# A transformer layer on one core: the maxima's small transfers issued from ScalarE instead of SyncE

## The chip, the core and the metric

The kernel runs on one core of a Trainium2 chip. The engines named here are TensorE (PE in the profile; PEld is its weight load), VectorE (DVE), ScalarE (ACT), GpSimd (POOL) and SyncE (SP), which in this kernel does nothing but issue DMA transfers. The metric is the device time of one execution in microseconds (us).

## The reference

One layer: attention, then a feed-forward product with quantised weights, each behind a layer norm and with a residual. The input is x of 4 x 512 x 1024 in float32.

```python
q = (h @ Wq).reshape(b, s, 32, 32)            # h = layernorm(x)
kv = h @ Wkv                                  # one key and value head of 32 for all query heads
scores = einsum('bqhd,bkd->bhqk', q, k) * 32**-0.5
scores = where(causal, scores + slopes * (pos_k - pos_q), -inf)
x = x + einsum('bhqk,bkd->bqhd', softmax(scores), v).reshape(b, s, 1024) @ Wo
w = (unpack_6bit(qweight) - zero_point) * scale
x = x + layernorm(x) @ w.T + ffn_bias
```

The softmax is what matters here. Per batch and head, the maximum of each query's row of scores is subtracted before the exponential.

## The kernel before, in words

**Tiling.** The 32 heads are taken in 8 groups of 4, and with 4 batches that makes 32 groups of work, i = 0 to 31. Each group passes through three functions. `queries` (L675) multiplies the normed input with the group's weights (matmuls at L682 into the tile pq), splits the result in a high and a low part (qh on ScalarE, ql on VectorE, L412 and L415), writes both to DRAM (q_d) and loads them back, turned, into the group's query stack, the tile qs: 96 rows of query parts, then 28 rows of bias terms (from qr_d), then two rows for the maxima. All of these transfers go through the helper `move` at L420, and SyncE issues them.

**Maxima.** `maxima` (L727) multiplies the first 124 rows of the stack with the keys (tile s, L739). VectorE takes the maximum of each row (L752, into mx). TensorE turns mx over (tile trm, L768). ScalarE copies it into mt (L774), which is the high part; VectorE subtracts that from trm for the low part (L779, a tile also shown as mt). Two transfers of 8 KB (qs<-mt) put these 16 x 128 values as rows 124 and 125 into the query stack. The keys hold -1 in these rows, so the second score matmul subtracts the maximum by itself.

**Attention.** `attention` (L798) multiplies keys with the whole stack of 126 rows (tile st, L820, eleven banks a group, two banks in turn), ScalarE takes the exponential (tile p, L830), GpSimd cuts off what lies behind the diagonal (L839) and adds up the blocks of keys (L861), TensorE multiplies with the values (pav, L849) and sums the denominators (den, L878). The first score matmul of a group cannot begin before both mt transfers of that group have landed.

**After attention**, from about 540 us, the 16 token tiles go through the output projection (po, L1048), the second layer norm and the feed-forward product (pf, L1168).

**The order.** All operations are first recorded as `Work` items with an engine, an estimated cost, a wished time and their dependencies. `order` lays them out on the engines by these costs, forward and backward, several times, and keeps the layout with the earliest estimated end; each engine then gets its instructions in that order and runs them strictly one after the other. A change of one cost or one engine can thus move instructions everywhere. For a transfer, `done` inside `forward` takes `ISSUE` (SP 450 ns, POOL 650 ns) off the issuing engine's time, puts the bytes on one shared DMA timeline, and counts the landing `DMA_LAT` (2000 ns) after its place on it. These are figures of the planner, not measurements. `move` always issues from SyncE:

```python
def move(dst, src):
    return nc.sync.dma_start(out=dst.bitcast(F32), in_=src.bitcast(F32))
```

Of the kernel before, what the change touches and what calls it, by code (L numbers as in the profile page):

```python
# [32 lines left out]
F32 = mybir.dt.float32  # L33
# [21 lines left out]
R_MAX = R_BIAS + N_BIAS  # L55
# [63 lines left out]
class Work:  # L119
# [2 lines left out]

    LAT = {"PE": 250, "ACT": 170, "DVE": 170, "POOL": 170, "SP": 0}
    SAME = {"PE": 0, "ACT": 150, "DVE": 110, "POOL": 110, "SP": 0}
    ISSUE = {"SP": 450, "POOL": 650}
    DMA_LAT = 2000
    EARLY = 12e3
    TURN = 105
# [119 lines left out]
    def forward(self, wanted, hold=None):  # L248

        n = len(self.ops)  # L250
        seen = [0.0] * n
        mine = [0.0] * n
        shared = {"dma": 0.0, "port": 0.0}

        def first(o):
            t = max(o.hold, hold[o.n] - self.EARLY) if o.size and hold else o.hold
            for m in o.before:
                a = self.ops[m]
                t = max(t, mine[m] if a.eng == o.eng and not a.size else seen[m])
            return t  # L260

        def done(o, s):
            if o.size:
                free = s + self.ISSUE[o.eng]
                shared["dma"] = max(shared["dma"], free) + o.size / self.DMA_RATE
                seen[o.n] = shared["dma"] + self.DMA_LAT
                return free
            if o.port:
                if o.eng == "DVE":
                    s = max(s, shared["port"])  # L270
                else:
                    shared["port"] = s + o.cost
            mine[o.n] = s + o.cost + self.SAME[o.eng]
            seen[o.n] = s + o.cost + o.lat
            return s + o.cost

        edges = [[] for _ in self.ops]
        for o in self.ops:
            for m in o.before:
                edges[m].append(o.n)  # L280
        start = self.line(edges, first, wanted, done)
        self.edges = edges
        return start, max(seen)

    def backward(self, start):
# [4 lines left out]
        def takes(o):  # L290
            return self.ISSUE[o.eng] if o.size else o.cost

# [49 lines left out]
def layer_kernel(  # L342
# [14 lines left out]
    nc = tc.nc  # L357
    B = x.shape[0]
    NT = S // P
# [21 lines left out]
    def new(pool_name, tag, shape, dt, name):  # L381

        p, bufs = pools[pool_name]
        return work.item(lambda: p.tile(shape, dt, tag=tag, name=name), (pool_name + tag, bufs))
# [8 lines left out]
    def pe(at, cols, fn, out, ins, more=0.0, tiled=False):  # L393

        o = work.op("PE", at, sum(c / 2.4 + 14.0 for c in cols) + more, fn, out, ins)
        o.wt, o.tiled = len(cols), tiled

    def act(at, n, fn, out, ins, sbuf=False):
        work.op("ACT", at, n / 1.2 + (90.0 if sbuf else 70.0), fn, out, ins)

    def dve(at, n, fn, out, ins, port=False, more=0.0):
        work.op("DVE", at, n / 0.96 + 75.0 + more, fn, out, ins, port=port)
# [4 lines left out]
    def dma(at, size, fn, out, ins, eng="SP"):  # L407
        work.op(eng, at, 0.0, fn, out, ins, size=size)
# [7 lines left out]
            [lo_it], [src_it, hi_it], port=port,  # L416
        )

    def move(dst, src):
        return nc.sync.dma_start(out=dst.bitcast(F32), in_=src.bitcast(F32))  # L420


    qr_d = tc.dram_tile([NG, N_BIAS, GH, S], F32R, name="qr_d")
# [19 lines left out]
        out=mask(),  # L443
        in_=mask(),
# [230 lines left out]
    def queries(at, i):  # L675
# [18 lines left out]
        for s, src in enumerate((qh, ql)):  # L694
            dma(
                at + 0.6 + 0.7 * s, 262e3,
                lambda s=s, src=src: move(q_d[i % 4, s], src()), [q_i[i % 4][s]], [src],
            )
        for h, n, q in qs[i]:
            dma(  # L700
                at + 1.0, 57e3 * n,
                lambda h=h, n=n, q=q: move(q()[R_BIAS:R_MAX, :, :], qr_d[g, :, h : h + n, :]),
                [(q, "b")], [qr_i[g]],
            )
            for r in range(3):
                dma(
                    at + 3.0 + 0.1 * r, 65e3 * n,
                    lambda r=r, h=h, n=n, q=q: move(
                        q()[ts(r, HD), :, :],
                        q_d[i % 4, r % 2, h * HD : (h + n) * HD].rearrange(  # L710
                            "(h d) q -> d h q", d=HD
                        ),
                    ),
                    [(q, r)], [q_i[i % 4][r % 2]],
                )

    def part(i, h):

        return next((q, h - first) for first, n, q in qs[i] if first <= h < first + n)
# [7 lines left out]
    def maxima(at, i):  # L727
        b = i // NG
        k = kst[b % 2]
        mx = new("small", "mx", [P, GH * NT], F32, f"mx_{i}")  # L730
        for n, bank in enumerate(S_BANKS):
            ps = new("ps_s", "s", [P, S], F32, f"s_{i}_{n}")
            widths = [(t + 1) * P for t, _ in bank]
            places = [sum(widths[:m]) for m in range(len(bank))]

            def products(ps=ps, bank=bank, widths=widths, places=places):
                for (t, h), W, o in zip(bank, widths, places):
                    q, at = part(i, h)
                    nc.tensor.matmul(  # L739
                        ps()[:, o : o + W], q()[0:R_MAX, at, ts(t, P)], k()[0:R_MAX, :W],  # L740
                        start=True, stop=True,
                    )
            pe(
                at + 1.2 * n, widths, products, [ps],
                [(q, r) for q in {part(i, h)[0] for _, h in bank} for r in ROWS] + [k],
                more=sum(45.0 if w == P else 5.0 for w in widths),
            )
            for (t, h), W, o in zip(bank, widths, places):
                junk = new("q1", "junk", [P, S], F32, f"junk_{i}_{t}_{h}")
                dve(  # L750
                    at + 1.2 * n + 0.3, W,
                    lambda ps=ps, junk=junk, t=t, h=h, W=W, o=o: nc.vector.tensor_tensor_reduce(  # L752
                        out=junk()[:, :W],
                        in0=ps()[:, o : o + W],
                        in1=mask()[:, S - W :],
                        scale=1.0,
                        scalar=-3e38,
                        op0=ALU.add,
                        op1=ALU.max,
                        accum_out=mx()[:, h * NT + t : h * NT + t + 1],  # L760
                    ),
                    [(mx, (t, h))], [ps], more=125.0,
                )
        at += 1.2 * len(S_BANKS)
        N = GH * NT
        tr = new("ps_misc", "misc", [P, P], F32, f"trm_{i}")
        pe(
            at, [P], lambda: nc.tensor.transpose(tr()[0:N, :], mx(), ident()), [tr], [mx]  # L768
        )
        for s in range(2):  # L770
            m = new("mt", f"mt{s}", [N, P], F32R, f"mt{s}_{i}")
            if s == 0:
                hi = m
                act(at + 0.2, P, lambda: nc.scalar.copy(hi(), tr()[0:N, :]), [hi], [tr])  # L774
            else:
                lo = m
                dve(
                    at + 0.4, P,
                    lambda: nc.vector.tensor_tensor(  # L779
                        lo(), tr()[0:N, :], hi().bitcast(F32), ALU.subtract  # L780
                    ),
                    [lo], [tr, hi],
                )
            for h, n, q in qs[i]:
                dma(
                    at + 0.5 + 0.2 * s, 2e3 * n,
                    lambda m=m, s=s, h=h, n=n, q=q: move(
                        q()[R_MAX + s : R_MAX + s + 1, :, :], m()[h * NT : (h + n) * NT, :]
                    ),
                    [(q, f"m{s}")], [m],  # L790
                )


# [436 lines left out]
    for b in range(B):  # L1230
        T = T0 + b * NG * STEP
        if b:
            for t in range(NT):
                load_x(T - 3.0 * STEP + 3.0 * t, b, t)
            for t in range(NT):
                layernorm(T - 2.0 * STEP + 3.0 * t, b, t)
        for c in range(KC):
            chunk(
                T - 4.0 + 0.5 * c if b == 0 else T - 0.9 * STEP + 1.3 * c - 2.6, b, c
            )  # L1240
        keys_values(T + 6.0 if b == 0 else T - 1.0, b)
        for g in range(NG):
            i = b * NG + g
            at = T0 + i * STEP
            queries(at, i)
            maxima(at + 17.0, i)
            attention(at + 34.0, i)
        invert(T + NG * STEP + 48.0, b)
# [52 lines left out]
```

## Time and profile before

| | us |
|---|---|
| median of 3 timed runs | 828.68 (827.39 to 829.8) |
| the profiled execution, whole | 830.86 |
| its span | 828.9 |
| TensorE busy in the span | 802.1 (97%) |
| VectorE, ScalarE, GpSimd busy | 572.4, 369.4, 515.7 |
| mt transfers, count and duration of an issue | 64, median 0.514 |
| score matmuls (L820), exponentials (L830) | 352 each |

The span runs from the first to the last instruction of the program; the whole execution has a little more around it. Busy shares are of the span. A matmul's duration is counted to its modelled end, so that successive matmuls overlap: those of 512 columns take 0.39 to 0.40 us each by their rows, and follow each other every 0.23 us. A TensorE that is busy 97% of the time is therefore not working at its peak for 97% of it. SyncE's rows (SPq) are the issues of transfers; the duration of such a row is the time that the issue holds SyncE, not the transfer itself. The clock row (PEclk) tells which share of full speed TensorE was granted.

### The profile page before, as it was taken

What the parts mean: (1) busy time and instruction counts of PE and PEld (TensorE: products, weight loads), DVE (VectorE), ACT (ScalarE), POOL (GpSimd) and SP (SyncE); (2) the same over time, 40 slices, a digit from 0 to 9 for tenths busy, and PEclk for the clock granted to TensorE, in tenths of its full rate; (3) what the DMA queues carried; (4) which work ended last, traced back from release to release, by engine and by line L of the source; (5) the groups of instructions that cost most, each with busy time, mean ns of one, the idle gap of its engine ahead of it and who ended that gap; (6) DMA issues with size and microseconds to landing.
All of it is one profiled execution on the core that took longest, in us unless ns stands there. A gap on an engine that the chain in (4) does not pass through costs nothing.

```text
span 828.9 us, 13434 instructions
## 1 busy us (share of the span) xinstructions
PE 802.1 (97%) x4480; PEld 595.8 (72%) x4480; DVE 572.4 (69%) x1491; ACT 369.4 (45%) x659; POOL 515.7 (62%) x442
## 2 busy tenths in 40 slices
PE   5989999999999999999999999999999999999997
PEld 5766677776566767666766667667888888888885
DVE  7576876478676469866358656645988867678755
ACT  4336664545665354755365564340142323333320
POOL 4337968285968185876388997778556445554323
PEclk9989999999999999999999999999999999999999
DMA  7997662486742397463457774626975675565321
GB/s 221 245 249 214 186 173 63 123 221 216 207 112 82 91 257 227 116 162 113 153 138 220 200 215 141 232 51 165 254 169 137 138 184 127 137 164 131 102 51 51
DMA packets 131796, 133.39 MB, mean 161 GB/s; under 512 B 42964, under 2 KB 93140, under 8 KB 130704
## 3 DMA queue, kind: packets, MB, share of 16 engines
q1 hardware_dynamic: 130912, 129.01, 57.4%
q0 software_dynamic: 816, 3.53, 1.5%
q8 instruction: 35, 0.57, 0.3%
q14 instruction: 33, 0.27, 0.1%
HBM read 85.58 MB, written 39.85 MB: 151 GB/s over the span
## 4 chain that ended last, share of the span: by engine, by line
PE 87%; DMA 4%; DVE 4%; issue 2%; POOL 1%; ACT 1%; SPq 0%; DVEq 0%; ACTq 0%; POOLq 0%
PE po L1048 21%; PE pq L682 18%; PE pf L1168 13%; PE s L739 9%; PE st L820 9%; PE pav L849 8%; PE den L878 3%; PE pkv L616 2%; PE tr L598 2%; DVE junk L752 2%; POOL p L861 1%; DMA q_d<-ql 1%; DMA qs<-q_d 1%; ACT p L830 1%; DMA qs<-qr_d 1%
## 5 line engine op out<-in xcount | busy, mean ns | idle before, releaser
L752 DVE CUSTOM_DVE_ANT_0 junk<-s,mask 128x256 f32<-128x256 f32 (+3 forms) x512 | 250.4, 489 | 123.2 <-PE s L739 92.1
L861 POOL TENSOR_TENSOR p<-p,p 128x1536 f32<-128x1536 f32 (+2 forms) x96 | 230.4, 2400 | 20.2 <-PE pav L849 18.2
L830 ACT ACTIVATE p<-st 128x512 f32<-128x512 f32 (+1 forms) x352 | 184.0, 560 | 115.1 <-PE st L820 111.7
L682 PE MATMUL pq<-xc,wqh 128*128 128x512 f32 x512 | 195.8, 402 | 1.5 <-DVE ql L415 1.4
L1048 PE MATMUL po<-woh,aT 128*128 128x512 f32 x512 | 165.7, 390 | 0.0
L839 POOL TENSOR_SCALAR_AFFINE_SELECT p<-p 128x512 f32<-128x512 f32 x128 | 81.9, 645 | 104.4 <-ACT p L830 103.7
L739 PE MATMUL s<-kst,qs 124*128 124x256 f32 (+3 forms) x512 | 138.4, 339 | 7.0 <-DVE mx L752 3.3
L820 PE MATMUL st<-qs,kst 126*128 126x512 f32 (+1 forms) x352 | 125.6, 395 | 3.1 <-ACT p L830 2.6
L1168 PE MATMUL pf<-wf,xT 128*128 128x512 f32 x512 | 120.8, 390 | 0.7 <-DVE xT L415 0.7
L739 PEld LDWEIGHTS s<-kst,qs 124*128 124x128 f32 x512 | 89.0, 193 | 44.1 <-DVE mx L752 16.3
L682 PEld LDWEIGHTS pq<-xc,wqh 128*128 128x128 f32 x512 | 97.6, 191 | 21.6 <-DVE ql L415 2.1
L1048 PEld LDWEIGHTS po<-woh,aT 128*128 128x128 f32 x512 | 96.2, 188 | 21.4 <-ACT a L867 0.8
L1168 PEld LDWEIGHTS pf<-wf,xT 128*128 128x128 f32 x512 | 95.8, 188 | 21.5 <-DVE xT L415 1.7
L682 PE MATMUL pq<-xc,wql 128*128 128x512 f32 x256 | 101.6, 397 | 0.0
L1048 PE MATMUL po<-wol,aT 128*128 128x512 f32 x256 | 99.7, 390 | 0.0
L820 PEld LDWEIGHTS st<-qs,kst 126*128 126x128 f32 x352 | 65.0, 190 | 24.1 <-ACT p L830 9.7
L849 PE MATMUL pav<-p,kv 128*32 128x512 f32 (+3 forms) x1024 | 79.4, 436 | 0.4 <-POOL p L839 0.4
L849 PEld LDWEIGHTS pav<-p,kv 128*32 128x32 f32 x1024 | 29.9, 109 | 50.7 <-issue 38.0
L1188 POOL TENSOR_TENSOR x<-x,y 128x512 f32<-128x512 f32 x30 | 43.0, 1438 | 26.4 <-DVE y L1179 26.4
L1048 PEld LDWEIGHTS po<-wol,aT 128*128 128x128 f32 x256 | 48.1, 188 | 9.6
L1146 POOL TENSOR_TENSOR x<-x,rows 128x512 f32<-128x512 f32 x32 | 43.9, 1391 | 17.3 <-issue 10.1
L682 PEld LDWEIGHTS pq<-xc,wql 128*128 128x128 f32 x256 | 49.0, 191 | 5.8
(92 smaller groups left out, 850.5 us busy)
## 6 DMA issues: line engine op xcount, KB each, us to landing
qs<-q_d SPq DMA_DIRECT2D x96, 256.0 KB
x<-_attn_hidden_states_dram SPq DMA_DIRECT2D x31, 512.0 KB
q_d<-qh SPq DMA_DIRECT2D x32, 256.0 KB
q_d<-ql SPq DMA_DIRECT2D x32, 256.0 KB
at_d<-a SPq DMA_DIRECT2D x32, 256.0 KB
raw<-at_d SPq DMA_DIRECT2D x16, 512.0 KB
raw<-rden_d SPq DMA_DIRECT2D x64, 128.0 KB
out_dram<-x SPq DMA_DIRECT2D x32, 256.0 KB
```

The source lines that it names most:

```text
L682: nc.tensor.matmul(pq(), w()[:, c, :], xc[b, c]()[:, s, :], start=(c == 0 and n == 0), stop=(c == KC - 1 and n == 2),)
L739: nc.tensor.matmul(ps()[:, o : o + W], q()[0:R_MAX, at, ts(t, P)], k()[0:R_MAX, :W], start=True, stop=True,)
L752: lambda ps=ps, junk=junk, t=t, h=h, W=W, o=o: nc.vector.tensor_tensor_reduce(out=junk()[:, :W], in0=ps()[:, o : o + W], in1=mask()[:, S - ...
L820: nc.tensor.matmul(ps()[:, place, :], k()[0:R_ALL, ts(j, P)], q()[0:R_ALL, mine, j * P :], start=True, stop=True,)
L830: lambda ps=ps, own=own, j=j: nc.scalar.activation(pr[j]()[:, own, :], ps(), AF.Exp),
L839: nc.gpsimd.affine_select(out=d, in_=d, pattern=[[0, GH], [1, P]], compare_op=ALU.is_ge, fill=0.0, base=0, channel_multiplier=-1,)
L849: nc.tensor.matmul(pav()[ts(h, HD), j * P :], kv[b]()[:, j, HD:], pr[j]()[:, h, :], start=(j == 0), stop=(j == NT - 1), tile_position=(0, ...
L861: nc.gpsimd.tensor_tensor(d, d, pr[j](), ALU.add)
L1048: nc.tensor.matmul(po(), aT[s][1]()[:, c, :], w()[:, ts(n, HALF)], start=(c == 0 and m == 0), stop=(c == KC - 1 and m == 2),)
L1146: nc.gpsimd.tensor_tensor(d, d, rows["bias"][n][1](), ALU.add)
L1168: nc.tensor.matmul(pf(), xT()[:, s, c, :], wf[c]()[:, ts(n, HALF)], start=(c == 0 and s == 0), stop=(c == KC - 1 and s == 1),)
L1188: (nc.vector if last else nc.gpsimd).tensor_tensor(d, d, y(), ALU.add)
```

## The change

The two mt transfers of each group are issued by ScalarE. `move` gets an argument for the engine, `maxima` passes ScalarE, and the recorded item has the engine ACT, so that it takes a place in ScalarE's order. The planner gets an issue cost for ScalarE (450 ns), and counts such a transfer's landing from the end of its issue, without the shared DMA timeline.

```diff
-    ISSUE = {"SP": 450, "POOL": 650}
+    ISSUE = {"SP": 450, "POOL": 650, "ACT": 450}
...
             if o.size:
                 free = s + self.ISSUE[o.eng]
+                if o.eng == "ACT":
+                    seen[o.n] = free + o.size / self.DMA_RATE + self.DMA_LAT
+                    return free
                 shared["dma"] = max(shared["dma"], free) + o.size / self.DMA_RATE
...
-    def move(dst, src):
-        return nc.sync.dma_start(out=dst.bitcast(F32), in_=src.bitcast(F32))
+    def move(dst, src, eng=None):
+        return (eng or nc.sync).dma_start(out=dst.bitcast(F32), in_=src.bitcast(F32))
...
                     lambda m=m, s=s, h=h, n=n, q=q: move(
-                        q()[R_MAX + s : R_MAX + s + 1, :, :], m()[h * NT : (h + n) * NT, :]
+                        q()[R_MAX + s : R_MAX + s + 1, :, :], m()[h * NT : (h + n) * NT, :],
+                        nc.scalar,
                     ),
-                    [(q, f"m{s}")], [m],
+                    [(q, f"m{s}")], [m], eng="ACT",
```

In the built program, ScalarE has 64 instructions more and SyncE 64 fewer; TensorE, VectorE and GpSimd have the same instructions as before, in another order.

## The prediction

> **What bounds the kernel now.** I read the page's slices first, to see which engine is full in which stage.
>
> ```profile
> PE   5989999999999999999999999999999999999997
> ...
> ACT  4336664545665354755365564340142323333320
> ...
> PEclk9989999999999999999999999999999999999999
> DMA  7997662486742397463457774626975675565321
> ```
>
> TensorE is full from the third slice to the last. ScalarE is at about half in the attention stage (46 to 540 us). TensorE's clock and load dip only near slice 3 and slice 11. The second view was the busy time by windows, to price those dips.
>
> ```profile
> core 0: us, PE busy (x) PEld busy (x) DVE busy (x) ACT busy (x) POOL busy (x), PEclk, DMA share, GB/s
> ...
> 46.00:60.00 14.00, 11.88 (x38) 8.29 (x37) 9.73 (x39) 3.46 (x6) 3.90 (x6) 0.76 0.98 289
> ...
> 220.00:232.00 12.00, 10.89 (x64) 7.51 (x57) 6.90 (x29) 5.53 (x8) 9.77 (x11) 0.86 0.58 185
> 232.00:540.00 308.00, 303.36 (x1928) 210.57 (x1927) 204.92 (x707) 166.51 (x327) 221.17 (x172) 1.00 0.58 164
> 540.00:828.90 288.90, 282.77 (x1295) 229.67 (x1293) 207.18 (x259) 80.36 (x107) 149.49 (x119) 1.00 0.54 133
> ```
>
> From 540 us on nothing of the change exists; that third of the span can move only through a new order of the instructions. In the rest TensorE lacks 2.1 us in the first dip, 1.1 us in the second and about 1.5% elsewhere. In the dips the granted clock is 0.76 and 0.86, which takes another 14.0 x 0.24 = 3.4 us and 12.0 x 0.14 = 1.7 us.
>
> Third, all instructions on the tile mt, which holds the maxima:
>
> ```profile
> L420 SPq DMA_DIRECT2D qs<-mt x64: 502/514/1622, 47.3 to 534.2; - x64
> L774 ACT CAST mt<-trm x32: 236/250/256, 45.9 to 533.4; 16x128 fp32r<-16x128 f32 x32
> L779 DVE TENSOR_TENSOR mt<-trm,mt x32: 226/274/279, 46.3 to 533.8; 16x128 fp32r<-16x128 f32 x32
> ...
>   PE st L820: 0.3, 1
> ```
>
> One issue costs its queue 0.514 us. The last line is a transfer's whole list of waiters that matters here: one score matmul, once, 0.3 us. Fourth, that place in order of time, with the chain's line for the transfer:
>
> ```profile
> 217.93 0.24 ACT L774 CAST mt<-trm 16x128 fp32r<-16x128 f32 x1
> ...
> 218.95 0.27 DVE L779 TENSOR_TENSOR mt<-trm,mt 16x128 fp32r<-16x128 f32 x1
> ...
> 219.18 0.53 SPq L420 DMA_DIRECT2D qs<-mt  x1
> ...
> 219.81 1.00 SPq L420 DMA_DIRECT2D qs<-q_d  x2
> ...
> 220.91 0.51 SPq L420 DMA_DIRECT2D qs<-mt  x1
> ...
> 226.06 0.70 PE L820 MATMUL st<-qs,kst 126*128 126x512 f32 x2 [0.31 <-DMA qs<-mt]
> ```
> ```profile
> 220.91 5.02 DMA qs<-mt
> ```
>
> Here two loads of 256 KB went onto SyncE's queue before the 8 KB of the second transfer, which took 5.02 us to land. That is the second dip. Last, who waits for ScalarE's exponentials and for what SyncE waits:
>
> ```profile
>   PEld st L820: 9.7, 25
>   PE st L820: 2.6, 7
> ```
> ```profile
> SPq L420 <- ACT mt L774: 44.8, 14, 9.8
> ```
>
> **The change part by part.** Profiled execution: span 828.9 us, 830.86 us in all, so 2.0 us lie around the span; it stands 2.2 us above the median of the three timed runs, 828.68 us. I work on the span and shift by the difference.
>
> *Taken off SyncE:* 64 issues x 0.514 = 32.9 us, and the 44.8 us (14 times) for which SyncE stood waiting for the copy that fills mt. In the old order on SyncE, the instruction after the second transfer is a load of q_d rows for the next stack in 17 of 32 groups. TensorE waits for those loads once, 0.7 us, and for the bias rows twice, 0.7 us. The work that hides the rest is the matmuls themselves. Gain between 0 and 1.4 us; I take 0, since these loads are issued a whole group ahead. In the new order SyncE is also passed by x and weight loads that the planner moves; they are priced with the order below.
>
> *Put on ScalarE:* the same 64 issues, 32.9 us beside 268.9 us of work in a 494 us window (46 to 540): 54% becomes 61%. In the new order the second issue follows the first directly in 18 of 32 groups, so ScalarE stands there until VectorE's subtraction (0.27 us) is done, which the first issue's own 0.51 us covers when VectorE is free. Behind the second issue stand an exponential (14 groups), a copy of qh (5), of a weight (4), of pav (3) or other copies. Who waits for a late exponential is the score matmul two banks on: now 32 of 352, of which 7 reach TensorE itself. If the same share of issue time reaches TensorE, 7/352 x 32.9 = 0.7 us, or 32/352 x 32.9 = 3.0 us by the weight loads. As most issues have other ScalarE slack (it waits 111.7 us for score matmuls), the bounds are 0 and 3.0 us if an issue costs there what it costs on SyncE; I take 1.2, nearer the lower row because 2.6 of the 12.3 us of waits reached the matmuls.
>
> *The landing.* From issue to the sixteenth completion event, the 64 transfers took 1.77 us at the least, 2.6 in the median and 6.3 at most; the second of each group 3.1 us in the mean. They are short where SyncE's queue is empty and long behind 256 KB loads. On ScalarE's own queue nothing large stands ahead, which the trace of before cannot show: bounds 1.77 and the 3.1 of SyncE. I take 2.6. The Trainium skill ("DMA: Bandwidth & Descriptors", Issuing engines are not separate DMA queues) speaks against this: transfers of all issuing engines share sixteen DMA engines and interleave, so only sequencer time is saved. By that rule the first two gains below are nought and the sum ends at about +1.9 us, the first rival. The 5.02 us row, with DMA at a share of 0.58, leans to waiting in one's own queue.
>
> *The order.* The planner prices the ScalarE transfer without the shared queue and moves work: by the built order, the matmuls between the transpose of the maxima and the first score matmul of the group, priced by the trace's start-to-start spacing (0.228 us for 512 columns, 0.176 for 384, 0.108 to 0.118 below, 0.04 to 0.11 for the tiled ones), sum to 5.9 us in the mean before and 5.1 after. The chain from transpose to rows is copy 0.29, issue 0.51, a second issue after 0.05, and its landing: 0.85 + 2.6 = 3.45 us. Three of 32 groups have less room, 0.8 us short in all. With each group's old landing instead (0.85 + 1.8 to 6.3) the new order is 13.1 us short. Take 0.8; bounds 0 and 13.1.
>
> *First dip.* For group 0 the order puts 3.1 us of matmuls instead of 4.8 before the first score matmul, and the rows, which took 5.5 us behind SyncE's loads, could be there some 3 us sooner, to fill idle time and keep the clock up. Worth between 0 (the start is bound by DMA, share 0.98) and 2.1 + 3.4 = 5.5 us; I take 3.0. *Second dip:* between 0 and 1.1 + 1.7 = 2.8 us; I take 2.0, as its cause is exactly the moved transfer.
>
> *Sum:* -3.0 - 2.0 + 0.8 + 1.2 = -3.0 us: span 825.9, profiled execution 827.9, and on the scale of the median 828.68 - 3.0 = 825.7 us. The reshuffle of the rest has no row. Waits of weight loads and matmuls on other engines come to about 1.5 us a group; if a tenth of that moves, it is 32 x 0.15 = 4.8 us either way, an estimate.
>
> **The rivals.** *Hidden anyway:* only 0.3 us is waited for on these transfers, and the start is bound by bytes. Dips stay, costs 1.9 us: 830.6 us, within the 0.3% (2.5 us) that a measurement of this kernel can tell from no change. For it: that single waiter. Against: the 5.02 us in the chain.
>
> *Rows late in a tighter order:* room fell by 0.8 us a group. If ScalarE's queue lands as SyncE's does, 13.1 us by the order; the old trace took 1.6 us more from transpose to scores than the order's sum (7.6 against 5.9), which would leave 3.2. Middle 8, no gains, plus 1.2: 838 us. It decides once the mean landing of the second transfer stays above 2.6 us. Against: the separate queue.
>
> *ScalarE becomes late (slower):* SyncE spends 172 of the 494 us issuing, and 30 issues take over 0.7 us, up to 1.84. If an issue on ScalarE must wait for one under way on SyncE, it costs perhaps 0.9 us instead of 0.514: 58 us on ScalarE. At a fifth reaching TensorE (2.6 of 12.3) that is 12 us, less the 5.0 gained and plus 0.8: 836 us. It decides from some 0.6 us an issue. The Trainium skill ("Perfetto Trace Analysis", DMA Instruction — HWDGE (DVE, Sync)) says that the descriptor generator is locked for exclusive use and that the lock wait lies inside the profiled issue, which speaks for this rival; no row of before shows ScalarE issuing.
>
> **How the numbers follow.** Forecast 0.44, hidden 0.22, late rows 0.15, late ScalarE 0.19. The forecast's own range is 820 to 826.2 (all bounds of the dips: -8.3 + 2.0, less part of the reshuffle). Eight in ten needs both signs: 819.5 leaves out one in fourteen below, 838 about one in eight above. Faster 0.44, same 0.22, slower 0.34.
>
> **What would show it.** Right: qs<-mt issued by ACT at about 0.5 us, landings near 2 us, PEclk near 1.00 in 46 to 60 and 220 to 232, waits of st on ACT p not above 16 us. Wrong: issue times of 0.8 us and more on ACT; st waiting for DMA qs<-mt by several us; the clock dips moved elsewhere by the new order. The last would make the prediction wrong without any of my steps being so.

## The result, and the profile after

The changed kernel takes 855.85 us (median; 851.65 to 856.77) against 828.88 us: a ratio of 1.032, with a 95% interval of 1.028 to 1.036. It is 27 us slower, where 825.7 us was forecast. The profiled execution takes 855.54 us with a span of 853.6 us, 24.7 us more than the span before; the numbers below account for that span.

The engine and clock slices of the page:

```profile
PE   5878999999899999999899989999899999999997
...
ACT  4425764446664454754355555330042232242320
...
PEclk9989999999999999999899999999999999999999
DMA  7878553376742467643376784535746565546531
```

ScalarE is as busy as before (371.7 us; 369.4 before). TensorE has more slices that are not full than before. The waits of TensorE, longest in total first (in total, times, longest of one; the score matmuls stand at L824 now):

```profile
PE st L824 <- DMA qs<-mt: 21.9, 11, 5.1
PE tr L601 <- DVE x L572: 7.6, 1, 7.6
PE pf L1172 <- DVE xT L418: 4.8, 2, 4.2
PE st L824 <- ACT p L834: 2.6, 7, 0.5
```

Here is the loss: score matmuls wait 21.9 us for the moved transfers, where they waited 0.3. The second line is the start of the kernel and stands in both (7.8 us before). The exponentials make the score matmuls wait 2.6 us, as before. The first of these places in order of time, and then the transfers on the chain that ended last:

```profile
48.35 0.28 DVE L782 TENSOR_TENSOR mt<-trm,mt 16x128 fp32r<-16x128 f32 x1
48.66 1.24 ACTq L423 DMA_DIRECT2D qs<-mt  x2
...
55.88 0.76 PE L824 MATMUL st<-qs,kst 126*128 126x512 f32 x1 [5.11 <-DMA qs<-mt]
```
```profile
49.36 6.39 DMA qs<-mt
68.14 5.37 DMA qs<-mt
183.37 4.33 DMA qs<-mt
227.66 4.80 DMA qs<-mt
...
407.34 5.80 DMA qs<-mt
...
503.14 5.12 DMA qs<-mt
```

ScalarE issues one directly after the other, as soon as VectorE has its part, but the second lands only 6.39 us after its issue. Eleven such transfers make 6.6% of the chain; before it was one. All instructions on mt:

```profile
L423 ACTq DMA_DIRECT2D qs<-mt x64: 510/511/967, 48.7 to 553.6; - x64
```

An issue costs ScalarE 0.511 us, as it cost SyncE 0.514. What the stalls do to the clock shows in the busy time by windows (the columns are as in the window view before):

```profile
50.00:62.00 12.00, 6.89 (x24) 5.37 (x22) 5.41 (x22) 3.35 (x6) 1.02 (x2) 0.72 0.61 182
68.00:80.00 12.00, 9.50 (x54) 7.41 (x51) 6.39 (x23) 4.91 (x8) 8.26 (x6) 0.86 1.03 287
408.00:420.00 12.00, 9.73 (x48) 7.34 (x47) 2.00 (x11) 4.63 (x9) 4.49 (x4) 0.72 0.45 125
502.00:514.00 12.00, 9.71 (x39) 7.42 (x38) 7.76 (x24) 6.29 (x12) 9.81 (x7) 0.86 0.73 227
604.00:616.00 12.00, 7.80 (x28) 6.00 (x27) 11.56 (x14) 1.04 (x1) 5.08 (x3) 0.86 0.49 162
```

In four windows a stall for mt of 2.3 us or more ends in TensorE's clock at half or is followed by it, 3.4 or 6.8 us long; in the fifth it is the 4.2 us wait for xT. By the clock's records the time at half speed, without the one at the very end of both kernels, sums to 23.9 us (10.2 before), so 11.9 us are lost to it instead of 5.1. The length of a stall alone does not decide it in these runs: a stall of 1.9 us was followed by such a stretch (at 99 us in the order of before issued by ScalarE, below), one of 2.4 us was not (at 506 us in the run without the three lines).

The account of the span: TensorE's gaps over 60 ns sum to 44.5 us, 22.8 more than before (21.7), of which 21.6 for mt; the clock takes 6.8 more. That is 29.6 of a measured 24.7. Of the 4.9 us over, about 0.7 are counted twice, since 1.8 us of the time at half speed lie inside the stalls (0.3 before); the rest is saved in smaller things that I have not taken apart.

### The profile page after: what moved, and what is told of

The parts are those of the page before. It is cut to its first block, busy times and chain, and to the rows that moved or that the text cites. A ratio compares the mean times of both kernels' runs of the same rounds, so it can differ in the third digit from the quotient of the medians.

```text
span 853.6 us, 13446 instructions
## 1 busy us (share of the span) xinstructions
PE 804.2 (94%) x4480; PEld 597.6 (70%) x4480; DVE 559.4 (66%) x1491; ACT 371.7 (44%) x659; POOL 521.4 (61%) x442
## 4 chain that ended last, share of the span: by engine, by line
PE 79%; DMA 12%; DVE 4%; issue 2%; ACT 2%; POOL 1%; SPq 0%; ACTq 0%; DVEq 0%; POOLq 0%
PE po L1052 18%; PE pq L685 16%; PE pf L1172 12%; PE st L824 9%; PE s L742 9%; PE pav L853 7%; DMA qs<-mt 7%; PE den L882 3%; PE pkv L619 2%; PE tr L601 2%; DMA qs<-q_d 2%; DVE junk L755 1%; DMA rows<-n_weight_zero_point_dram 1%; DMA qw<-in_L_ffn_qweight_dram 1%; ACT p L834 1%
## 5 line engine op out<-in xcount | busy, mean ns | idle before, releaser
L685 PE MATMUL pq<-xc,wqh 128*128 128x512 f32 x512 | 197.8, 403 | 1.9 <-DVE ql L418 1.2
L824 PE MATMUL st<-qs,kst 126*128 126x512 f32 (+1 forms) x352 | 128.9, 405 | 24.5 <-DMA qs<-mt 21.9
L1172 PE MATMUL pf<-wf,xT 128*128 128x512 f32 x512 | 123.5, 394 | 4.8 <-DVE xT L418 4.8
L824 PEld LDWEIGHTS st<-qs,kst 126*128 126x128 f32 x352 | 65.7, 195 | 49.6 <-issue 16.0
L1150 POOL TENSOR_TENSOR x<-x,rows 128x512 f32<-128x512 f32 x32 | 47.7, 1510 | 16.1 <-issue 9.8
```

Source lines behind the costliest of these rows:

```text
L685: nc.tensor.matmul(pq(), w()[:, c, :], xc[b, c]()[:, s, :], start=(c == 0 and n == 0), stop=(c == KC - 1 and n == 2),)
L824: nc.tensor.matmul(ps()[:, place, :], k()[0:R_ALL, ts(j, P)], q()[0:R_ALL, mine, j * P :], start=True, stop=True,)
L1150: nc.gpsimd.tensor_tensor(d, d, rows["bias"][n][1](), ALU.add)
L1172: nc.tensor.matmul(pf(), xT()[:, s, c, :], wf[c]()[:, ts(n, HALF)], start=(c == 0 and s == 0), stop=(c == KC - 1 and s == 1),)
```

## The experiments

Theory A: the new order leaves too little room between the transpose of the maxima and the group's first score matmul, and the rows land late from whichever queue. Theory B: the issues hold ScalarE. Theory C: ScalarE's queue itself is slower. Others are named where they come up. "Landing" is the time from a transfer's issue to its sixteenth completion event in the trace, as in the prediction; "room" is the prediction's sum over the built order. Before stood at 828.6 to 830.4 us (median) in these comparisons; each ratio is against the executions of before on the same chip.

**The changed kernel's order, issued by SyncE.** All engines keep the order of the changed kernel; the 64 transfers take the same places, on SyncE.

```diff
-                        nc.scalar,
+                        nc.sync,
```

> The changed kernel's order on every engine, but the 64 transfers are issued by SyncE at the places the order gives them. Theory A (the new order leaves too little room before the first score matmul of a group, and the rows land late from whichever queue): still slow, 848 to 858 us, score matmuls waiting for the mt transfers by 15 us or more. Theory B (the issues hold ScalarE): back to 826 to 834 us. Theory C (ScalarE's queue lands later than SyncE's by itself): the waits of the score matmuls fall below 8 us and the time to about 838 us.

Measured: 859.37 us, ratio 1.036 (1.034 to 1.039). Its waits of TensorE:

```profile
PE st L824 <- DMA qs<-mt: 22.1, 12, 3.5
```

The loss does not need ScalarE: with the order kept and the issuing engine put back, the wait is the same 22 us, and theory B fails. The mean landing is 3.0 us from SyncE and 3.6 us from ScalarE in this order. But SyncE comes to its second issue later, 2.3 us after the start of the transpose of the maxima instead of 1.9, so that both rows are in place 5.5 us after it in the mean in either run. In the kernel before they were in place after 5.2 us. What changed more is the work that hides this time: between that transpose and the first score matmul, its waits taken out, TensorE has 6.5 us of work a group in the trace, where it had 7.7 before.

**The order of before, issued by ScalarE.**

```diff
-    def move(dst, src):
-        return nc.sync.dma_start(
+    def move(dst, src, eng=None):
+        return (eng or nc.sync).dma_start(
...
-                        q()[R_MAX + s : R_MAX + s + 1, :, :], m()[h * NT : (h + n) * NT, :]
+                        q()[R_MAX + s : R_MAX + s + 1, :, :], m()[h * NT : (h + n) * NT, :],
+                        nc.scalar,
```

> The order of before on every engine, but the 64 transfers are issued by ScalarE at the places they had. Theory A: close to before, 827 to 835 us, the score matmuls waiting for the mt transfers by less than 4 us. Theory B: most of the loss is here, 845 us or more, with exponentials late and score matmuls waiting for them. Theory C: waits of the score matmuls for the transfers of 8 us and more, about 840 us.

Measured: 832.98 us, ratio 1.006 (1.003 to 1.008). TensorE's waits:

```profile
PE st L821 <- DMA qs<-mt: 3.2, 3, 1.9
PE st L821 <- ACT p L831: 1.9, 6, 0.7
```

The engine alone costs 4 us, and not because ScalarE is late: the wait for exponentials is 1.9 us (2.6 before). The wait for mt is 2.9 us longer; the mean landing is 3.3 us instead of 3.0. So the engine makes a few of the 27 us at most, the order the rest; theory B falls, and theory C as the main cause.

**The planner's three lines alone.** The transfers stay on SyncE and are planned on SyncE; only their landing is counted without the shared DMA timeline.

```diff
                 free = s + self.ISSUE[o.eng]
+                if o.size == 8e3:
+                    seen[o.n] = free + o.size / self.DMA_RATE + self.DMA_LAT
+                    return free
                 shared["dma"] = max(shared["dma"], free) + o.size / self.DMA_RATE
```

> The transfers stay on SyncE; only the planner's three lines are there, so that it counts their landing 2.0 us after the issue, without the shared DMA timeline. The room by the order is 5.4 us a group. Theory A (the planner's landing makes the loss, whoever issues): 838 to 856 us, score matmuls waiting for the mt transfers by 10 us or more. Theory D (the loss needs ScalarE's issue places in the plan, and is the luck of one order): 826 to 836 us.

Measured: 852.86 us, ratio 1.028 (1.024 to 1.031).

```profile
PE st L823 <- DMA qs<-mt: 12.3, 7, 3.4
PE tr L601 <- DVE x L572: 8.1, 1, 8.1
PE s L742 <- DVE mx L755: 6.2, 6, 4.2
PE pf L1171 <- DVE xT L418: 2.8, 2, 2.1
```

Without any ScalarE issue, the planner's belief about the landing makes nearly the same loss, about half of it in direct waits for mt, and the clock takes 11.9 us (5.1 before). Theory D expected 826 to 836 us and fails here.

**The three lines left out, ScalarE kept.**

```diff
-                if o.eng == "ACT":
-                    seen[o.n] = free + o.size / self.DMA_RATE + self.DMA_LAT
-                    return free
```

> The change with the planner's three lines on the landing left out: transfers are issued by ScalarE, and their landing is counted on the shared DMA timeline as in the kernel before. The room before the first score matmul is 6.2 us a group by the order instead of 5.1. Theory A: 826 to 838 us, waits for the mt transfers below 8 us. Theory B: 848 us or more, as in the changed kernel.

Measured: 843.14 us, ratio 1.017 (1.014 to 1.019). A part miss. The wait for mt is 3.8 us as expected, and the clock takes 5.1 us, as before, but the time stays 14.5 us above before:

```profile
PE s L739 <- DVE mx L752: 5.5, 9, 1.3
PE st L821 <- DMA qs<-mt: 3.8, 4, 1.5
PE st L821 <- ACT p L831: 3.5, 9, 0.7
PE s L739 <- DMA q_d<-qh: 2.4, 1, 2.4
```

These are other small waits of a new order; all gaps sum to 30.8 us (21.7 before). They cover 9 of the 12 us by which the span grew.

**A later landing in the plan.** The landing is counted from the end of the issue, in three sizes; the first is the changed kernel.

```diff
-                    seen[o.n] = free + o.size / self.DMA_RATE + self.DMA_LAT
+                    seen[o.n] = free + o.size / self.DMA_RATE + 2.25 * self.DMA_LAT
```

With a factor of 2.25 (4.5 us):

> The change with the planner's landing for these transfers at 4.5 us after the issue instead of 2.0. The room is 6.8 us a group by the order. Theory A: waits for the mt transfers below 5 us, 824 to 836 us. Theory B: 848 us or more.

With 1.6 (3.2 us):

> The change with the planner's landing at 3.2 us after the issue instead of 2.0 (855.9 us) or 4.5 (826.7 us). Room 6.0 us a group by the order. Theory A: between them, 828 to 845 us, waits for the mt transfers 3 to 12 us and at least one dip of the clock. Theory D: anywhere from 824 to 855 us, without relation to the waits for these transfers.

The factor of 2.25 once more, and 3.0 (6.0 us):

> The same kernel as with the 4.5 us landing, with more rounds. Theory A: 824 to 829 us, 0.1 to 0.5% below before. Theory D (luck of one set of runs): the interval takes in 1.

> The change with the planner's landing at 6.0 us after the issue. Room 7.9 us a group by the order. Theory A: waits for the mt transfers below 1 us and no dip of the clock before the end; 822 to 832 us, as there is little left to gain over the 4.5 us landing.

| planned landing | room by the order | wait for mt | median, ratio |
|---|---|---|---|
| 2.0 us (the change) | 5.1 us | 21.9 us | 855.9, 1.032 (1.028 to 1.036) |
| 3.2 us | 6.0 us | 4.9 us | 839.8, 1.013 (1.009 to 1.017) |
| 4.5 us | 6.8 us | 0.8 us | 826.7, 0.998 (0.996 to 0.9995) |
| the same again | 6.8 us | 2.2 us | 828.0, 0.997 (0.995 to 0.998) |
| 6.0 us | 7.9 us | 0.0 us | 845.2, 1.018 (1.014 to 1.021) |

Up to 4.5 us this is as theory A has it, and the version at 4.5 us is a little faster than before, by 0.2 and 0.3%. In its first profile the clock stays full in both old dips:

```profile
46.00:60.00 14.00, 12.35 (x55) 9.18 (x54) 11.30 (x46) 4.65 (x10) 4.62 (x7) 1.00 1.01 255
220.00:232.00 12.00, 11.83 (x73) 8.49 (x72) 10.45 (x33) 8.43 (x15) 8.98 (x11) 1.00 0.40 106
```

In the profile of the second set the first dip is back (6.8 us at half speed), with a profiled time of 830.25 us. The 6.0 us landing missed its expectation: TensorE does not wait for mt, and it is slower by 1.8%. TensorE waits more for VectorE's maxima, for bias rows and for exponentials (3.3, 0.7 and 2.6 us before):

```profile
PE s L742 <- DVE mx L755: 5.3, 12, 1.2
PE s L742 <- DMA qs<-qr_d: 4.3, 8, 1.9
PE st L824 <- ACT p L834: 3.9, 8, 1.1
```

The profiled execution is the fastest of the six (839.41 us), so these lines do not cover the whole of the 1.8%. Why the planner's order is worse there is not settled; TensorE's wait for mt is not the cause. So the luck of an order that theory D speaks of exists, at about 2%, beside the effect of these waits.

**The same room with SyncE.** First planned on SyncE with the 4.5 us landing, then the order of the 4.5 us version with the transfers put on SyncE.

```diff
+                if o.size == 8e3:
+                    seen[o.n] = free + o.size / self.DMA_RATE + 2.25 * self.DMA_LAT
+                    return free
```

> The transfers stay on SyncE, and the planner counts their landing 4.5 us after the issue, without the shared timeline. Room 7.0 us a group by the order. Theory A: 823 to 834 us, waits for the mt transfers below 4 us: the room is worth as much with SyncE as with ScalarE. Theory E (what made the late landing with ScalarE's issue 2 us faster than before is that SyncE was freed): 829 us or more.

```diff
-                        nc.scalar,
+                        nc.sync,
```

> The order of the run with the 4.5 us landing on every engine, its 64 transfers issued by SyncE at the same places. Theory A: 825 to 832 us; with this much room the issuing engine hardly matters, either way by less than 5 us. Theory E: 832 us or more.

Measured: 832.19 us, ratio 1.003 (1.000 to 1.005), and 834.47 us, ratio 1.005 (1.002 to 1.007). The waits for mt are 0.6 and 1.6 us in the profiled executions, which are the fastest and the second fastest of their ten (826.91 and 830.18 us): with this room TensorE hardly waits for the transfers from either queue, as theory A has it. But the second, with the same order as the 826.7 us version, is some 7 us slower against before on its own chip, which is outside what theory A expected. There the matmuls of `maxima` wait for SyncE's loads of q_d rows, which is no wait of the 826.7 us version:

```profile
PE s L742 <- DMA qs<-q_d: 3.0, 2, 1.8
```

So taking the issues off SyncE is worth some 7 us in this order, which was planned for it, and costs 4 in the order of before, which was planned for SyncE. In the order of the changed kernel it may be worth 3.5 us (859.4 against 855.9), but the intervals of the two ratios overlap. Theory E's expectation is met in both runs (theory A's in the first alone); it stands for this version.

**Does ScalarE's queue go by SyncE's bytes?** In the 4.5 us version, SyncE issues one more transfer of 512 KB at the moment of each group's first mt transfer.

```diff
-                    lambda m=m, s=s, h=h, n=n, q=q: move(
-                        q()[R_MAX + s : R_MAX + s + 1, :, :], m()[h * NT : (h + n) * NT, :],
-                        nc.scalar,
+                    lambda m=m, s=s, h=h, n=n, q=q: (
+                        s == 0 and nc.sync.dma_start(
+                            out=load_d[i],
+                            in_=m().bitcast(F32).unsqueeze(1).to_broadcast([16, 64, P]),
+                        ),
+                        move(
+                            q()[R_MAX + s : R_MAX + s + 1, :, :], m()[h * NT : (h + n) * NT, :],
+                            nc.scalar,
+                        ),
                     ),
```

> The kernel with the 4.5 us landing, and at each group's first mt transfer, which ScalarE issues, SyncE issues one more transfer of 512 KB (the same 16 x 128 values, 64 times over, into a DRAM buffer that nobody reads). Theory A (ScalarE's transfers share the DMA engines with SyncE's bytes and wait behind them): the mean landing of the 64 mt transfers rises from 3.3 us to 4.5 us or more, and score matmuls wait for them by 8 us or more. Theory F (ScalarE's queue goes by SyncE's bytes): the landing stays below 3.8 us and the waits below 3 us.

Measured: 958.4 us. The first mt transfer of a group, issued together with the load, lands after 3.7 us in the mean (3.2 without the load); the second, issued after it, after 7.6 us (3.4 without the load). The instructions on mt and the waits:

```profile
L423 ACTq DMA_DIRECT2D qs<-mt x64: 510/519/3555, 48.8 to 656.8; - x64
...
L792 SPq DMA_DIRECT2D load_d<-mt x32: 563/568/3051, 48.8 to 656.0; - x32
```
```profile
PE st L831 <- DMA qs<-mt: 34.3, 17, 4.2
PE s L743 <- DMA qs<-q_d: 13.8, 5, 5.9
```

ScalarE's transfers land later behind SyncE's bytes; theory F falls. Of the 7.6 us, 4.9 pass before the transfer's first packet moves, and its issue is over after 0.9 in the mean; whether the time between goes by in making the descriptors or at the DMA engines, no run tells. The changed kernel's own 64 landings say the same, sorted by the KB that SyncE issued from 2.5 us before to 0.7 us after each (sizes from the page, transposes at their tile's 256 KB): nothing issued, 12 transfers, 1.8 us in the mean; under 500 KB, 9, 2.2 us; 500 to 900 KB, 22, 3.4 us; more, 21, 5.3 us.

## Why the prediction was wrong, step by step

The step that failed is *The order*: its 0.8 us of waits for the rows were 21.9. With it failed the two dips, -5.0 us in the sum and +6.8 in the run. What the forecast allowed for ScalarE itself held.

*What bounds the kernel* was right: TensorE is full, and its stalls and its clock account for the time that was lost.

*Taken off SyncE*, taken as 0: in the order of before ScalarE's issue costs 4 us, in the order at 4.5 us it is worth 7; in the changed kernel's order 3.5, which is not clear of noise. The bounds of 0 to 1.4 us were too narrow.

*Put on ScalarE*, 0 to 3.0 us: held. The wait for exponentials is 2.6 us on the matmuls and 10.9 us on the weight loads (2.6 and 9.7 before), and an issue costs 0.511 us. (The second issue follows the first directly in 15 groups of the trace, not in 18.) So the rival of a late ScalarE is refuted. The Trainium skill ("Perfetto Trace Analysis", DMA Instruction — HWDGE (DVE, Sync)) puts the wait for the descriptor generator inside an issue. The trace can be read that way for three of the 64: the three issues on ScalarE that took over 0.7 us, up to 0.967, each ended within 0.1 us of the end of an issue of 1.06 to 1.38 us that SyncE had under way; the median shows nothing of it.

*The landing* failed too. I took 2.6 us, between 1.77 and 3.1; it is 3.6 us in the mean and 3.4 in the median, outside the bounds. The step read the 5.02 us row as waiting in SyncE's own queue. The load experiment and the sorted landings show that the transfers land later the more bytes SyncE has just issued, from ScalarE's queue as well. The rule of the Trainium skill that I weighed against it ("DMA: Bandwidth & Descriptors", Issuing engines are not separate DMA queues) was the better guide: its case was a gain of nought from the queue. Yet that case, too, ended at only +1.9 us (by its terms, 0.8 + 1.2, +2.0), and the landing alone is not the loss: with 3.0 us from SyncE the same order waits as long.

*The order* failed by size. I took 0.8 us of 0 to 13.1; the wait is 21.9 us. The groups' old landings were not an upper bound, since the new order also brings SyncE's loads closer to the maxima: 21 of 64 transfers had more than 900 KB issued around them, 6 in the kernel before. In the eleven groups that waited, the second transfer landed after 5.1 us in the mean (3.9 in the same groups before), where I counted a median for every group. The start of the chain was too short as well: I had 0.85 us from the transpose to the second issue, where the trace has 1.9 from the transpose's start (2.2 before, so the old trace already showed it); 0.6 us of it pass between ScalarE's copy and VectorE's subtraction. That makes 7.0 us until the rows are there in these groups, against 5.1 us of work that TensorE had to fill them; the eleven differences come to 20.5 of the 21.9 us.

*The dips*: I took -5.0 us. The first dip stayed, and behind stalls of 2.3 us and more new ones came, +6.8 us. No term of mine had a cost for a dip behind a new stall. That the dip at 220 to 232 us had exactly the moved transfer as its cause was read too boldly: before it TensorE waited 0.31 us for mt, but also three times, 0.26 to 0.27 us each, for VectorE's maxima. With the old order and ScalarE's issues it is gone, and another stands at 100 us; these are single profiles.

*The rivals.* "Rows late in a tighter order" was the right mechanism, with its point of decision (a mean landing of the second transfer above 2.6 us) passed at 3.6; I gave it 0.15 and a price of 838 us, short by 18: 8 us of waits instead of 21.9, and no clock. The reshuffle of 4.8 us either way was too small as well: orders without a noteworthy wait for mt ran from 826.7 to 845.2 us.

## What to carry to other kernels

Where a planner sets the order, a change of its model of one transfer can cost more than the transfer: ask first what latency the new order believes in, and check that against the landings of the trace under load, not at rest. A small transfer moved to another issuing engine can still land late behind the bytes that the first one issues. A stall on the bounding engine has a second price if its clock falls after it.

## What the runs showed that I had not expected

A planner that believes in later landings is not better without end: planned landings of 2.0, 3.2, 4.5 and 6.0 us gave 855.9, 839.8, 826.7 and 845.2 us, each with one order alone. An issue on ScalarE, 0.51 us in the median, took up to 3.56 us in the run with SyncE's extra 512 KB a group; in the changed kernel the longest was 0.97 us. And from the same order and places the 8 KB transfers took longer from issue to landing on ScalarE than on SyncE, 3.6 against 3.0 us and 3.3 against 3.0 us in the mean. Since ScalarE also issued them sooner, the rows were in place hardly later, 5.5 us after the start of the transpose from both in the changed kernel's order and 5.4 against 5.2 in that of before.
